# Row loads of two blocks, their normalization and one residual moved in a transformer block with routed experts

## The chip, the cores and the metric

The kernel runs on one core of a Trainium2 chip. The metric is the device time of one execution in microseconds (us). Three executions of the kernel before gave 1010.34, 1008.1 and 1010.42 us, median 1010.34. The profile comes from one further execution of 1009.59 us, whose span from the first to the last instruction is 1007.8 us.

Engines are named as the profile names them: PE (matrix multiplications and transposes), PEld (its weight loads), DVE, ACT and POOL (element-wise work), SP (which here only issues transfers). Each has a list of instructions of its own, in an order that the program fixes.

## The reference

The input x has 4 sequences of 1024 tokens with 256 features. All data are float32. What is computed, in short:

```python
z = layernorm(x)                      # the outer normalization
h = layer_norm(z)                     # ln1 of the attention
q, k, v = h @ wq, h @ wk, h @ wv      # 4 heads of 64
q = softmax(q * scale, axis=-1)       # over the features of a head
k = softmax(k * scale, axis=-2)       # over the 1024 tokens of a sequence
context = einsum('bhnd,bhne->bhde', k, v)
x1 = z + einsum('bhnd,bhde->bhne', q, context) @ wo + bo
x2 = x1 + gelu(layer_norm(x1) @ w_ff1 + b_ff1) @ w_ff2 + b_ff2
x3 = x + layernorm(x2 @ w_d + b_d)
# then: eight low-rank experts, two per token, on layernorm(x3);
out = x3 + layernorm(experts(rms_norm(layernorm(x3))))
```

The softmax of k runs over a whole sequence, so the context of a sequence needs all of its tokens.

## The kernel before, in words

**Tiling.** The 4096 tokens are cut into 8 blocks of 512 tokens; blocks 0 and 1 are the first sequence, 2 and 3 the second, and so on. A block is a tile of 128 partitions x 4 tokens x 256 features. Numbers at the end of a tile's name in this text are the block (z_2 is the tile z of block 2).

**Streams.** The program is written as Python generators, here called streams. `front(i)` takes the rows z_i of block i, normalizes them, transposes them (tiles pt_h, then hT), computes q and k (pq, pk), the exponentials, the transposes of q and k (pt_q, pkt) and the products of k with z (pz). At the second block of a sequence it makes the context and folds it into one matrix, mix (pzk, pctx, pmix). `middle(i)` loads the rows a second time (x_i, line 796), makes the normalized residual x1_i from them on ACT (line 806), multiplies q with mix (pa, line 821 adds it), and runs the feed-forward part (pf, py). `tail` makes the routing inputs. `prepare_q`, `prepare_attn`, `prepare_ff` and `prepare_ranks` prepare weights (for the second: pv, pw; for the third: pwt, pwdt, pbdt, pwdg, pwd, pbd, pbf, pc).

**What sets the order.** A planner in the program decides at build time which stream takes its next step. Each step adds to an estimated clock: `now()` for PE, `V`, `A`, `G` for DVE, ACT and POOL. A stream that yields a number waits until that estimated time; one that yields a function waits until the function is true. For data that come by transfer the planner holds estimates: the table `ARRIVE` for the first loads, and `now() + 2.5` for the later ones. What comes out is a fixed order of instructions on each engine. On the chip semaphores hold an instruction until its inputs are there, and everything behind it on that engine waits with it.

**Transfers.** SP issues the weights in this order: wff2 (line 201), wd, bd, wff1, w1 (1 MB each but wd and bd), eight pieces of b1 (line 185, 64 KB each), w3 (1 MB), eight pieces of b3, w2 (1 MB), eight pieces of b2; then the rows x_0 and x_1 of the residual (line 796, 512 KB each), and then, as buffers come free, z_2, x_2, x_3, z_3 and so on. The program gives the transfers of SP and ACT eight semaphores in turn, so a transfer is issued only when the one eight places before it has landed.

**Buffers.** Pool `zp` has two buffers for z, so z_2 is loaded (line 170) when z_0 is no longer needed, that is after pz_0; z_3 after pz_1. Pool `sp` has two buffers with the tag "row" that hold x_2 and x_3 in this phase. There are eight PSUM banks, handed out to the matrix products in turn by `psum`.

**Lines that matter below.** 351 to 369: normalization of z on DVE and ACT (POOL makes the reciprocal root, line 354). 611: copies to hT on ACT. 635: exponential of q. 657 and 658: maximum and copy of k. 672: exponential of k. 703 and 715: copies of the transposed q and k. 765: mix. 796, 806, 821: rows, normalized residual and sum in `middle`.

Of the kernel before, what the change touches and what calls it, by code (L numbers as in the profile page):

```python
# [15 lines left out]
P = 128  # L16
# [49 lines left out]
def sandwich_kernel(  # L66
# [98 lines left out]
        return ap[i * BLK : (i + 1) * BLK, :].rearrange("(p t) d -> p t d", t=TB)  # L165

    def load_z(i):
        zs[i] = zp.tile([P, TB, D], F32, tag="z", name=f"z_{i}")
        if i > 1:
            nc.sync.dma_start(out=zs[i], in_=tokens(x, i))  # L170
            return
        for t, eng in ((0, nc.sync), (HT, nc.scalar)):
            eng.dma_start(out=zs[i][:, t : t + HT, :], in_=tokens(x, i)[:, t : t + HT, :])
# [29 lines left out]
    nc.sync.dma_start(out=wd_s[:, :, 0:D], in_=wd.rearrange("(c p) f -> p c f", p=P))  # L203
    bd_s = wp.tile([P, DX], F32, tag="bd_s", name="bd_s")
    nc.sync.dma_start(out=bd_s[:, 0:D], in_=bd.partition_broadcast(P))
    wff1_s = load_w(nc.sync, wff1, [P, DC, FF], "wff1_s", "(c p) f -> p c f", p=P)
    w1_s = load_w(nc.sync, w1, [P, DC, FF], "w1_s", "(c p) f -> p c f", p=P)
    b1_s = load_ranks(b1, "b1_s")
    w3_s = load_w(nc.sync, w3, [P, DC, FF], "w3_s", "(c p) f -> p c f", p=P)
# [15 lines left out]
    def now():  # L225
        return pe[0] / 2400.0 + idle[0]
# [50 lines left out]
    def calm():  # L277

        return free["V"] - 0.5
# [130 lines left out]
        return read_out(e)  # L410


    ARRIVE = {"z0": 4.3, "z1": 9.1, "wqv": 8.6, "wff2": 14.6, "wff1": 18.0}

    def prepare_q():

# [55 lines left out]
    def prepare_ranks():  # L472
# [21 lines left out]
        for t, r_, n in ((a13_s.rearrange("p c (a k) -> p (c a) k", a=2),  # L494
# [6 lines left out]
                A(0.25 + n * STRIP / 1000.0)  # L501
            yield 0.0

    def prepare_ff():
        yield ARRIVE["wff2"]
        wff2T = mp1.tile([P, DC, FF], F32, tag="actB", name="wff2T")
        for c in range(DC):
            for h in range(2):
                pt = psum(f"pwt_{c}_{h}")
                for j in range(4):  # L510
                    flip(pt[:, j * P : (j + 1) * P], wff2_s[:, h * 4 + j, c * P : (c + 1) * P])
                nc.scalar.copy(wff2T[:, c, h * BLK : (h + 1) * BLK], pt)
                e = read_out(A(0.6, now() + 0.2))
                yield 0.0

        wdT = mp2.tile([P, DC, D], F32, tag="m1", name="wdT")
        bdT = mp2.tile([P, D], F32, tag="wt", name="bdT")
        pt = psum("pwdt")
        for e_ in range(DC):
            for c in range(DC):  # L520
                flip(pt[:, e_ * D + c * P : e_ * D + (c + 1) * P], wd_s[:, c, e_ * P : (e_ + 1) * P])
        nc.scalar.copy(wdT.rearrange("p e d -> p (e d)"), pt)
        read_out(A(0.6, now() + 0.2))
        pt = psum("pbdt")
        for c in range(DC):
            flip(pt[:, c * P : (c + 1) * P], bd_s[:, c * P : (c + 1) * P])
        nc.scalar.copy(bdT, pt[:, 0:D])
        e = read_out(A(0.45, now() + 0.2))
        yield e
        pw = psum("pwdg")  # L530
        for e_ in range(DC):
            g = wq_s[:, e_, D:DX]
            for c in range(DC):
                mm(pw[:, c * E : (c + 1) * E], wdT[:, e_, c * P : (c + 1) * P], g,
                   e_ == 0 and c == 0, False, skip_group_check=True)
            mm(pw[:, DC * E : (DC + 1) * E], bdT[:, e_ * P : (e_ + 1) * P], g, False, e_ == DC - 1,
               skip_group_check=True)
        nc.vector.tensor_copy(
            wd_s[:, :, D:DX], pw[:, 0 : DC * E].rearrange("p (c e) -> p c e", e=E)
        )  # L540
        nc.vector.tensor_copy(bd_s[:, D:DX], pw[:, DC * E : (DC + 1) * E])
        yield read_out(V(0.25, now() + 0.2))
        for f in range(FC):
            pw = psum(f"pwd_{f}")
            for c in range(DC):
                mm(pw[:, 0:DX], wff2T[:, c, f * P : (f + 1) * P], wd_s[:, c, :], c == 0, c == DC - 1)
            nc.vector.tensor_copy(wff2d_s[:, f, :], pw[:, 0:DX])
            read_out(V(0.4, now() + 0.2))
            yield 0.0

        pw = psum("pbd")
        for c in range(DC):
            mm(pw[:, 0:DX], vcol(V_BFF2, c).to_broadcast([P, P]), wd_s[:, c, :], c == 0, c == DC - 1)
        nc.vector.tensor_tensor(bd_s, bd_s, pw[:, 0:DX], ALU.add)
        read_out(V(0.4, now() + 0.2))
        yield 0.0
        yield ARRIVE["wff1"]

        pw = psum("pbf")
        for f in range(FC):  # L560
            for c in range(DC):
                mm(pw[:, f : f + 1], wff1_s[:, c, f * P : (f + 1) * P], vcol(V_LN2B, c),
                   c == 0, c == DC - 1)
        nc.vector.tensor_tensor(bff1_s, vec[:, V_BFF1 : V_BFF1 + FC], pw[:, 0:FC], ALU.add)
        read_out(V(0.15, now() + 0.2))
        for c in range(DC):
            nc.vector.tensor_scalar(
                wff1_s[:, c, :], wff1_s[:, c, :], vcol(V_LN2G, c), None, ALU.mult
            )
            yield V(1.2)  # L570
        for h in range(2):
            cols = slice(h * BLK, (h + 1) * BLK)
            centred([wff1_s[:, c, cols] for c in range(DC)], wff1_s, cols, f"pc1_{h}", 0.69)
            yield 0.0


    qTs, norms, mixes, kmaxes, ksums, kzs, xgs = {}, {}, {}, {}, {}, {}, {}
    summed, attended, stored = set(), set(), {}

    def front(i):  # L580
        b, h = divmod(i, BPB)

        def new(what, shape):


            pool, tag = {
                1: {"hT": (bp, "h2T"), "q": (mp1, "copy"), "k0": (gp, "g"), "k1": (gp, "g")},
                0: {},
            }.get(i if i < 2 else i % 2 * 3, {
                "hT": (mp2, "u0"), "q": (mp2, "tT"), "k0": (mp2, "act0"), "k1": (mp2, "act1"),  # L590
            }).get(what, (bp, what))
            return pool.tile(shape, F32, tag=tag, name=f"{what}_{i}")

        if i not in zs:
            load_z(i)
        z = zs[i]
        yield now() + 2.5 if i > 1 else ARRIVE[f"z{i}"]
        st, mv = tiles(f"in{i}")
        for js in ((0, 1), (2, 3)):
            stats(z, st, mv, js)  # L600
            yield calm()
        rr = small([P, TB], "rr", f"rr_x{i}", 3)
        yield rsqrt2(mv, 1e-5, 1e-5, rr, f"x{i}")
        norms[i] = mv
        yield lambda: i < 2 or i - 2 in summed
        lm, e = less_mean(mv, rr, f"z{i}")
        yield normalize(z, z, mv, rr, lm, e, "VAVA")
        hT = new("hT", [P, DC, BLK])

        def to_h(c, pt):  # L610
            nc.scalar.copy(hT[:, c, :], pt)

        yield from transposed(z, f"h{i}", to_h)
        yield lambda: zeroth.done

        q = new("q", [P, TB, DX])
# [20 lines left out]
            yield 0.0  # L637

        wide = small([P, TB], "wide", f"wide_{i}")
        nc.vector.reciprocal(wide, rr)  # L640
        yield lambda: i < 6 or 2 * i - 11 in turned
        xgs[i] = small([P, TB, E], "xg", f"xg_{i}", 6)
        nc.vector.tensor_tensor(
# [7 lines left out]
        for c in range(DC):  # L651
# [5 lines left out]
            nc.vector.tensor_reduce(kmax[:, c, h : h + 1], pk, AX.X, ALU.max)  # L657
            nc.scalar.copy(k, pk)
            read_out(max(V(0.7, now() + 0.2), A(0.6, now() + 0.2)))
            yield 0.0  # L660
        yield lambda: h == 0 or b in ksums

# [16 lines left out]
        else:  # L679
# [3 lines left out]
            nc.vector.tensor_tensor(less, kbias, kbias0, ALU.subtract)  # L683
            nc.scalar.activation(less, less, AF.Exp)
            e = A(0.2, V(0.15), "exp")
            nc.vector.tensor_tensor(ksum0, ksum0, less, ALU.mult)
            nc.vector.tensor_tensor(ksum, ksum, ksum0, ALU.add)
            nc.vector.reciprocal(ksum, ksum)
# [16 lines left out]
        for _ in transposed(q, f"q{i}", to_q):  # L705
            yield 0.0

        kt = new("q", [P, TB, D])
        for jj in range(0, TB, 2):
            pt = psum(f"pkt_{i}_{jj}")  # L710
# [5 lines left out]
            end = read_out(A(0.6, now() + 0.2))  # L716
            yield 0.0
        yield end
        yield lambda: h == 0 or i - 1 in summed
        pz = psum(f"pz_{i}")  # L720
        for c in range(DC):
            for n in range(TB):
# [70 lines left out]
    def middle(i):  # L793
# [1 line left out]
        xt = xts[i] = pool.tile([P, TB, RW], F32, tag=tag, name=f"x_{i}")  # L795
        nc.sync.dma_start(out=xt[:, :, 0:D], in_=tokens(x, i))
        yield now() + 2.5
        yield lambda: i // BPB in mixes and (i < 2 or i - 1 in flipped)
        qT, mix = qTs[i], mixes[i // BPB]
        _, r, e = rsqrt(norms[i], 1e-5, f"x{i}")  # L800
        pool, tag = (mp1, "actB") if i == 1 else (x1p, "x1")
        x1 = pool.tile([P, TB, D], F32, tag=tag, name=f"x1_{i}", bufs=1)
# [2 lines left out]
        for j in range(TB):  # L805
# [4 lines left out]
        nc.gpsimd.iota(xt[:, :, R_ID], pattern=[[1, TB]], base=i * BLK, channel_multiplier=TB,  # L810
                       allow_small_or_imprecise_dtypes=True)
        G(0.6)
        st, mv = tiles(f"x1_{i}")
        for jj in range(0, TB, 2):
            pa = psum(f"pa_{i}_{jj}")
# [11 lines left out]


        aside = {1: "u0", 3: "act", 5: "act"}.get(i)
        yield lambda: i < 2 or (i - 2 if i < 7 else i - 1) in fed  # L830
        yield lambda: aside != "act" or ranked.done

# [804 lines left out]

    EN = mybir.EngineType
    with tc.manual_schedule(engines={EN.PE, EN.DVE, EN.Activation, EN.Pool}):
        fronts = [  # L1640
            Stream(lambda i=i: i < 2 or i - 2 in summed,
                   lambda i=i: front(i))
            for i in range(NBLK)
        ]
        zeroth = Stream(always, prepare_q)
        first = Stream(always, prepare_attn)
        once = Stream(always, prepare_ff)
        ranked = Stream(always, prepare_ranks)
        blocks = [
            Stream(lambda i=i: i < 2 or (stored.get(AFTER[i]) == 2 if i in AFTER else i - 2 in attended),  # L1650
                   lambda i=i: middle(i))
            for i in range(NBLK)
        ]
# [13 lines left out]
        def sides():  # L1667

            yield from closing
            yield zeroth  # L1670
            yield from ready
            yield from tails
# [119 lines left out]
```

## Time and profile before

| what | value |
|---|---|
| profiled execution | 1009.59 us, span 1007.8 us |
| median of three executions | 1010.34 us |
| busy time of PE | 970.8 us (96%) |
| busy time of DVE, ACT, POOL | 452.2, 339.5, 416.6 us |
| PE busy in 0 to 36.49 us (up to the first pq of block 1) | 26.33 us |
| PE busy in 36.49 to 100 us | 57.76 of 63.51 us |
| PE busy in 100 to 330 us | 230.00 of 230.00 us |
| PE busy in 330 to 1007.8 us | 656.71 of 677.80 us |
| mean granted clock of PE | 0.991 |

How to read it: the row of a group gives the line of the kernel, the engine, the operation, the tile written and the tiles read, the count, the busy time and the idle time of the engine just before with what ended it. A row of the timeline begins with start and duration in us. "SPq" and "ACTq" are the transfer issues of those engines. PE's busy time counts also a matrix product that runs at half clock.

### The profile page before, as it was taken

The page shows a single profiled execution, that of the slowest core. Times are in us where ns is not written, and L with a number is a line of the kernel's source. Part 1 is how long each engine was busy: PE and PEld are TensorE (multiplying, and loading weights), DVE is VectorE, ACT ScalarE, POOL GpSimd, SP SyncE. Part 2 cuts the span into 40 slices and gives each one's busy share as a digit, 9 for nine tenths or more (in the row PEclk, how much of TensorE's full clock was granted, in tenths as well). Part 3 has the DMA queues.
Part 4 walks back from the last instruction along what each step waited for, and adds up shares of the span by engine and source line. Part 5 has one row for each costly group of instructions (what it writes and reads, how often), then busy time and mean ns, then how long its engine had stood idle before and what let it go on. Part 6 is the DMA issues. An engine that isn't in the chain of part 4 may idle for free. (4 is left out here: it accounts for less than half of the span.)

```text
span 1007.8 us, 12120 instructions
## 1 busy us (share of the span) xinstructions
PE 970.8 (96%) x4259; PEld 652.9 (65%) x4259; DVE 452.2 (45%) x1427; ACT 339.5 (34%) x702; POOL 416.6 (41%) x464
## 2 busy tenths in 40 slices
PE   6997999999999999998999999999999999999993
PEld 5776888888888888887764363543636446364453
DVE  5575575848574554745222324333233332332123
ACT  2424552353432222221213424345243442421110
POOL 2003001201212213232753847849387593866432
PEclk9999999999999999999999999999999999999997
DMA  8501800100202101121200110201111020100000
GB/s 286 180 22 31 189 26 22 59 27 1 86 3 83 44 19 47 65 70 31 68 10 0 43 44 26 64 6 49 37 43 43 0 65 1 43 32 21 1 0 23
DMA packets 30960, 48.01 MB, mean 48 GB/s; under 512 B 4176, under 2 KB 22704, under 8 KB 30896
## 3 DMA queue, kind: packets, MB, share of 16 engines
q1 hardware_dynamic: 20832, 32.15, 10.4%
q10 hardware_dynamic: 6992, 6.55, 2.7%
q0 software_dynamic: 3072, 8.51, 2.3%
q8 instruction: 35, 0.57, 0.2%
q14 instruction: 29, 0.24, 0.1%
HBM read 26.09 MB, written 17.17 MB: 43 GB/s over the span
## 5 line engine op out<-in xcount | busy, mean ns | idle before, releaser
L305 PE MATMUL ph<-tT,w_s 128*128 128x512 f32 (+1 forms) x576 | 235.6, 554 | 3.0 <-DVE act L1267 2.8
L305 PEld LDWEIGHTS ph<-tT,w_s 128*128 128x128 f32 x576 | 105.5, 190 | 124.8 <-issue 110.4
L305 PE MATMUL py<-wff2d,g 128*128 128x264 f32 x512 | 119.2, 386 | 0.0
L305 PEld LDWEIGHTS py<-wff2d,g 128*128 128x128 f32 x512 | 97.4, 190 | 16.5
L1267 DVE TENSOR_TENSOR act<-act,ph 128x512 f32<-128x512 f32 (+1 forms) x96 | 55.7, 595 | 104.2 <-PE ph L305 56.0
L1317 POOL TENSOR_TENSOR actA<-act,act 128x512 f32<-128x512 f32 x32 | 40.7, 1271 | 129.0 <-DVE act L1267 119.5
L1552 ACT COPY py<-ph 128x512 f32<-128x512 f32 x94 | 53.2, 571 | 120.5 <-PE ph L305 119.6
L305 PE MATMUL pf<-h2T,wff_s 128*128 128x256 f32 x384 | 87.1, 380 | 0.9 <-DVE h2T L854 0.9
L1259 ACT ACTIVATE act<-ph 128x512 f32<-128x512 f32 (+1 forms) x96 | 48.4, 521 | 115.1 <-PE ph L305 98.5
L305 PEld LDWEIGHTS pf<-h2T,wff_s 128*128 128x128 f32 x384 | 72.1, 190 | 12.4 <-issue 1.6
L1267 DVE TENSOR_TENSOR act<-act,py 128x512 f32<-128x512 f32 x48 | 32.9, 686 | 103.6 <-ACT act L1259 103.6
L879 ACT ACTIVATE g<-pf,bff 128x256 f32<-128x256 f32 x128 | 52.1, 475 | 72.8 <-PE pf L305 72.7
L305 PE MATMUL po<-w_s,actA 128*128 128x256 f32 x256 | 60.6, 384 | 0.6 <-ACT tT L1372 0.5
L904 DVE TENSOR_TENSOR y<-py,bd_s 128x264 f32<-128x264 f32 x32 | 13.8, 431 | 101.0 <-PE py L305 101.0
L305 PE MATMUL po<-w_s,actB 128*128 128x256 f32 x256 | 59.0, 379 | 0.0
L1078 POOL DMA_INDIRECT rows<-x,to x32 | 31.9, 998 | 63.9 <-DVE rsa_x L340 17.4
L305 PEld LDWEIGHTS po<-w_s,actA 128*128 128x128 f32 x256 | 46.9, 190 | 14.1 <-issue 7.2
L305 PEld LDWEIGHTS po<-w_s,actB 128*128 128x128 f32 x256 | 48.7, 190 | 11.2 <-issue 5.3
L305 PE MATMUL py<-u,bw 32*128 32x512 f32 x192 | 54.4, 640 | 0.0
L305 PE MATMUL ph<-u,bw 32*128 32x512 f32 x192 | 54.4, 640 | 0.0
L343 POOL TENSOR_TENSOR rs_y<-rsa_y,neghalf 128x2 f32<-128x2 f32 x16 | 11.4, 715 | 93.4 <-DVE rsa_y L340 86.2
L1317 POOL TENSOR_TENSOR actB<-act,act 128x512 f32<-128x512 f32 x31 | 39.6, 1278 | 21.9 <-DVE act L1267 21.9
(280 smaller groups left out, 1610.3 us busy)
## 6 DMA issues: line engine op xcount, KB each, us to landing
rows<-none ACTq DMA_DIRECT2D x4, 1052.0 KB, 13.9
kept<-x SPq DMA_DIRECT2D x8, 526.0 KB, 2.7
x<-in_x_dram SPq DMA_DIRECT2D x8, 512.0 KB, 3.8
row<-rows SPq DMA_DIRECT2D x7, 526.0 KB, 3.9
w_s<-in_w_dram SPq DMA_DIRECT2D x3, 1024.0 KB
z<-in_x_dram SPq DMA_DIRECT2D x6, 512.0 KB
bw<-b_s SPq DMA_DIRECT2D x24, 128.0 KB, 3.8
wff_s<-in_wff_dram SPq DMA_DIRECT2D x2, 1024.0 KB
```

Source lines behind the costliest of these rows:

```text
L305: nc.tensor.matmul(out_, lhsT=lhsT, rhs=rhs, start=start, stop=stop, **kw)
L343: nc.gpsimd.tensor_tensor(r, a, neghalf[:, 0:n], ALU.pow)
L879: nc.scalar.activation(g[:, k * W : (k + 1) * W], pf[:, k * W : (k + 1) * W], AF.Gelu_apprx_tanh, bias=bff1_s[:, f : f + 1],)
L904: nc.vector.tensor_tensor(y[:, j % HT, :], py[:, 0:DX], bd_s, ALU.add)
L1078: ins = nc.gpsimd.indirect_dma_start(out=dst[:, :], out_offset=bass.IndirectOffsetOnAxis(ap=at, axis=0), in_=src, in_offset=None, bounds_c ...
L1259: nc.scalar.activation(to, h, AF.Silu)
L1267: nc.vector.tensor_tensor(to, to, h3, ALU.mult)
L1317: lambda x0=x0, x1=x1, op=op: nc.gpsimd.tensor_tensor(ac, x0, x1, op))
L1552: nc.scalar.copy(py[a], ph[a])
```

## The change

1. `load_z(2)` and `load_z(3)` take the two "row" buffers of pool `sp` and are issued by SP in the prologue: z_2 ahead of wff1, z_3 ahead of w1. The planner's table gets the estimates 15.0 and 19.0 for them.
2. The normalization of z leaves `front` and becomes a stream of its own, `prelude(i)`. Blocks 1 to 3 are normalized by ACT alone ("AAAA"), with the product of mean and reciprocal root on POOL; blocks 0 and 4 to 7 stay with both engines ("VAVA").
3. `middle(i)` no longer waits for the context before it makes the normalized residual x1; it waits only for the statistics of the block (and an order among blocks), and asks for the context later, ahead of the products pa.
4. Some waits of the planner keep buffers safe in the new order (`keyed`, `folded`, `summed`).

```diff
     def load_z(i):
-        zs[i] = zp.tile([P, TB, D], F32, tag="z", name=f"z_{i}")
+        if i in (2, 3):
+            zs[i] = sp.tile([P, TB, RW], F32, tag="row", name=f"z_{i}")[:, :, 0:D]
+        else:
+            zs[i] = zp.tile([P, TB, D], F32, tag="z", name=f"z_{i}")
...
+    load_z(2)
     wff1_s = load_w(nc.sync, wff1, [P, DC, FF], "wff1_s", "(c p) f -> p c f", p=P)
+    load_z(3)
     w1_s = load_w(nc.sync, w1, [P, DC, FF], "w1_s", "(c p) f -> p c f", p=P)
...
-    ARRIVE = {"z0": 4.3, "z1": 9.1, "wqv": 8.6, "wff2": 14.6, "wff1": 18.0}
+    ARRIVE = {"z0": 4.3, "z1": 9.1, "wqv": 8.6, "wff2": 14.6, "z2": 15.0, "wff1": 18.0, "z3": 19.0}
...
+    def prelude(i):
+        if i not in zs:
+            load_z(i)
+        z = zs[i]
+        yield now() + 2.5 if i > 3 else ARRIVE[f"z{i}"]
+        st, mv = tiles(f"in{i}")
+        for js in ((0, 1), (2, 3)):
+            yield lambda: i < 2 or free["V"] < now() + 0.5
+            stats(z, st, mv, js)
+        rr = rrs[i] = small([P, TB], "rr", f"rr_x{i}", 3)
+        if 0 < i < 4:
+            lm = small([P, TB], "lm", f"lm_z{i}", 8)
+            nc.vector.tensor_scalar(lm, mv[:, :, 0], -1.0, None, ALU.mult)
+            V(0.15)
+            rsqrt2(mv, 1e-5, 1e-5, rr, f"x{i}")
+            nc.gpsimd.tensor_tensor(lm, lm, rr, ALU.mult)
+            e = G(0.5)
+            norms[i] = mv
+            yield lambda: 0 in heads if i == 1 else now() > e and free["A"] < now() + 1.5
+            zeds[i] = normalize(z, z, mv, rr, lm, e, "AAAA")
+        else:
+            yield rsqrt2(mv, 1e-5, 1e-5, rr, f"x{i}")
+            norms[i] = mv
+            yield lambda: i < 4 or i - 2 in summed
+            lm, e = less_mean(mv, rr, f"z{i}")
+            zeds[i] = normalize(z, z, mv, rr, lm, e, "VAVA")
...
     def middle(i):
...
         nc.sync.dma_start(out=xt[:, :, 0:D], in_=tokens(x, i))
         yield now() + 2.5
-        yield lambda: i // BPB in mixes and (i < 2 or i - 1 in flipped)
-        qT, mix = qTs[i], mixes[i // BPB]
+        yield lambda: i in norms and (i - 1 in flipped if i > 1 else i == 0 or folded)
         _, r, e = rsqrt(norms[i], 1e-5, f"x{i}")
...
         G(0.6)
+        yield lambda: i // BPB in mixes and i in qTs
+        qT, mix = qTs[i], mixes[i // BPB]
```

Lines of the changed kernel are later by 3 to 35: the residual's load is line 829, the residual line 838, the normalization line 380.

More of the change, by code (lines that the diff above doesn't have):

```diff
@@ L502, in prepare_ranks @@
             yield 0.0
+    folded = []
     def prepare_ff():
@@ L549, in prepare_ff @@
             yield 0.0
+        folded.append(True)
         pw = psum("pbd")
@@ L574, in prepare_ff @@
             yield 0.0
-    qTs, norms, mixes, kmaxes, ksums, kzs, xgs = {}, {}, {}, {}, {}, {}, {}
-    summed, attended, stored = set(), set(), {}
+    rrs, qTs, norms, mixes, kmaxes, ksums, kzs, xgs = {}, {}, {}, {}, {}, {}, {}, {}
+    keyed, summed, attended, stored = set(), set(), set(), {}
+    zeds, heads = {}, set()
+    def prelude(i):
[24 more added lines that the diff above has]
+            zeds[i] = normalize(z, z, mv, rr, lm, e, "VAVA")
     def front(i):
@@ L588, in new @@
                 0: {},
-            }.get(i if i < 2 else i % 2 * 3, {
+            }.get(i if i < 2 else 3 if i == 2 else i % 2 * 3, {
                 "hT": (mp2, "u0"), "q": (mp2, "tT"), "k0": (mp2, "act0"), "k1": (mp2, "act1"),
@@ L592, in new @@
             return pool.tile(shape, F32, tag=tag, name=f"{what}_{i}")
-        if i not in zs:
-            load_z(i)
+        yield lambda: i in zeds
         z = zs[i]
[L597 to L607, printed above, removed]
+        yield zeds[i]
         hT = new("hT", [P, DC, BLK])
@@ L611, in to_h @@
             nc.scalar.copy(hT[:, c, :], pt)
-        yield from transposed(z, f"h{i}", to_h)
+        for he in transposed(z, f"h{i}", to_h):
+            yield 0.0
+        heads.add(i)
+        yield he
         yield lambda: zeroth.done
@@ L639, in front @@
         wide = small([P, TB], "wide", f"wide_{i}")
-        nc.vector.reciprocal(wide, rr)
+        nc.vector.reciprocal(wide, rrs[i])
         yield lambda: i < 6 or 2 * i - 11 in turned
@@ L659, in front @@
             read_out(max(V(0.7, now() + 0.2), A(0.6, now() + 0.2)))
+            if c == DC - 1:
+                keyed.add(i)
             yield 0.0
@@ L685, in front @@
             e = A(0.2, V(0.15), "exp")
+            yield max(e, ke)
             nc.vector.tensor_tensor(ksum0, ksum0, less, ALU.mult)
@@ L706, in front @@
             yield 0.0
+        yield lambda: i != 3 or 2 in summed
         kt = new("q", [P, TB, D])
@@ L718, in front @@
         yield end
-        yield lambda: h == 0 or i - 1 in summed
+        yield lambda: i == 0 or i - 1 in summed
         pz = psum(f"pz_{i}")
@@ L829, in middle @@
         aside = {1: "u0", 3: "act", 5: "act"}.get(i)
+        yield lambda: aside != "u0" or 2 in keyed and 3 in summed
         yield lambda: i < 2 or (i - 2 if i < 7 else i - 1) in fed
@@ L1639, in sandwich_kernel @@
     with tc.manual_schedule(engines={EN.PE, EN.DVE, EN.Activation, EN.Pool}):
-        fronts = [
-            Stream(lambda i=i: i < 2 or i - 2 in summed,
-                   lambda i=i: front(i))
+        preludes = [
+            Stream(lambda i=i: i < 4 or i - 2 in summed, lambda i=i: prelude(i))
             for i in range(NBLK)
         ]
+        fronts = [Stream(always, lambda i=i: front(i)) for i in range(NBLK)]
         zeroth = Stream(always, prepare_q)
@@ L1649, in sandwich_kernel @@
         blocks = [
-            Stream(lambda i=i: i < 2 or (stored.get(AFTER[i]) == 2 if i in AFTER else i - 2 in attended),
+            Stream(lambda i=i: i < 2 or (stored.get(AFTER[i]) == 2 if i in AFTER else i - 2 in attended and i in summed),
                    lambda i=i: middle(i))
@@ L1669, in sides @@
             yield from closing
+            yield from preludes
             yield zeroth
```

## The prediction

> **What bounds the kernel now.** I read the share of busy time first, then PE's waits in the first 200 us, then busy time by stretch, then the timelines of SP and ACT. PE is busy 96% of the span.
>
> ```profile
> PE pcg L305 <- DVE gate_s L421: 8.7, 1, 8.7
> PE pt_h L318 <- DVE x L821: 4.1, 3, 1.4
> PE pt_q L318 <- DVE lm_x L360: 1.5, 1, 1.5
> PE pt_q L318 <- DVE lm_z L360: 1.4, 1, 1.4
> PE pmix L305 <- DVE cbd L757: 0.2, 1, 0.2
> ```
>
> These are PE's waits up to 200 us: in total, count, longest. The first is the start, which the change leaves alone. What it can win lies in the other four: 1.4 us at 26 us, and 4.1 + 1.5 + 0.2 = 5.8 us between 66 and 92 us. From 100 to 330 us PE has no idle time at all, and from the products pa of block 6 (329 us) PE's order is the same in both programs. The matrix instructions are the same in number and kind, and the array changes between whole, row and column use equally often. So the change is decided in the first stretch, and whatever PE loses there comes back nowhere: the end moves by the same amount.
>
> ```profile
> 11.02 10.28 SPq L185 DMA_DIRECT2D b_s<-in_b_dram  x8
> 21.34 0.42 SPq L177 DMA_DIRECT2D w_s<-in_w_dram  x1
> 21.81 6.55 SPq L185 DMA_DIRECT2D b_s<-in_b_dram  x8
> 28.48 1.44 SPq L177 DMA_DIRECT2D w_s<-in_w_dram  x1
> 29.96 5.80 SPq L185 DMA_DIRECT2D b_s<-in_b_dram  x8
> 35.81 1.35 SPq L796 DMA_DIRECT2D x<-in_x_dram  x2
> ```
>
> These are SP's issues. The residual's rows x_0 go out last, at 35.81 us, behind three weights of 1 MB and 24 small pieces. The trace's landing times for x are 3.8/5.5/7.3 us (least, median, most); x_0 is the first in an empty queue (1 to 5% DMA share at 35 to 37 us), so it lands at about 35.8 + 3.8 = 39.6.
>
> ```profile
> 20.23 0.63 ACT L635 ACTIVATE q<-q 128x512 f32<-128x512 f32 x1 [4.66 <-DVE q L631]
> ...
> 31.69 1.16 ACT L611 COPY hT<-pt_h 128x512 f32<-128x512 f32 x2
> ...
> 79.34 2.08 ACT L806 ACTIVATE x<-x,lm_x,rs_x 128x256 f32<-128x256 f32 x4 [2.21 <-DVE lm_x L360]
> ```
>
> ACT reads x_0 only at 79.34 us, 40 us after it landed, so that late load costs nothing before.
>
> **The moved residual.** In the changed program's order x1_0 (line 838) stands on ACT right behind the normalization of z_1, ahead of the exponentials of q_0, the copies and exponentials of k_0, the copies to hT_1, and all that follows. Its first instruction waits for the load of x_0, which SP still issues last. The planner counted 2.5 us for that load. ACT's order in the built program:
>
> ```
> 15 L380 Activation z_1_193<-z_1_193,lm_z1_317,rr_x1_316 128x256 x4
> 16 L838 Activation x1_0_286<-x_0_258,lm_x0_347,rs_x0_283 128x256 x4
> 17 L664 Activation q_0_354<-q_0_354 128x2x256 x2
> 18 L687 TensorCopy k0_0_387<-pk_0_0_388 128x512
> ```
>
> When does ACT get there? DVE ends the statistics of z_1 at 14.4; POOL's root takes 1.05 (line 354), its product perhaps 0.5 (an estimate between the iota's 0.14 and that root); four normalizations make 2.1, as the four of line 806 do: ACT is free at 18.4, with these steps' gaps of some 0.3.
>
> When does x_0 land? SP's small pieces each wait for an earlier transfer. The last of b1 goes out at 20.99, when w1 has landed; the last of b3 when w3 has (28.05); the last of b2 when w2 has (35.45); then x_0. The two new loads add 1.05 MB ahead of w1, while the queue moves 330 to 430 GB/s (8 to 18 us): 2.7 us. The chain behind keeps its lengths, so x_0 is issued at 38.5 and lands at 42.3. ACT stands from 18.4 to 42.3.
>
> What waits? After that ACT needs 2.1 for x1_0, 1.2 for two exponentials of q (0.63 each), 1.1 for two copies of k, 1.5 for its exponentials (24.74 to 26.26 before), 1.1 for the copies to hT_1: 7.0 us, and 0.2 to PE. The first pq of block 1 starts at 49.5. PE can do pq_0, pk_0, pt_h_1, pw and most of the weight transposes until 27.4 and then has nothing. DVE stands too, at the sums of q_0.
>
> How far behind is PE then? Before, pq of block 1 started at 36.5. But PE had by then also done pt_q_0 (0.90), pkt_0 (0.88), pwdg (1.25), two pwd (1.78) and pz_0 (3.46), by the differences of their starts: 8.3 us that the changed order has still ahead. So the lag is 49.5 - 36.5 + 8.3 = **21.3 us**, with the 1.4 us stall at 26 us contained in it.
>
> **What the rest wins and adds.** The other 5.8 us of stalls go: x1_0 is made long before its products, and z_2 and z_3 are at hand. New close pairs come: pmix_0 directly ahead of pa_0, where DVE's mix must come between (0.88 us, line 765, and the way there and back: 1.3); pkt_3 directly ahead of pz_3, with a copy between (0.8); pz_3 one product ahead of pzk_1, with DVE's sum between (0.4). Together +2.5. By bounds these may be 0, or as much as before (5.8).
>
> The clock: before, PE's granted clock is 0.50 for 3.4 us twice, at 53.8 (after pbf, 32 products with one column) and at 91.3 (after the stalls at 88 to 92); each costs 1.7. The second goes with its stalls, -1.7; pbf stays. After 22 us of idle PE starts cold. The row for that is the start of the profile: from 8.75 to 16.3 us pcg, pbq, pv, pt_h and pw take some 7.6 us, about twice what the same forms take later (eight pt_h 1.95 against 1.06, four products with 256 columns 1.75 against 1.03): a loss of up to 3.9. The two dips lost 1.7. I take 2.5, since some of the cold stretch falls on weight transposes still ahead of hT_1; bounds 0 and 3.9.
>
> The Trainium skill, "TensorE: Matmul & The Clock Gate", Part 1, gives one activity window of about 3.4 us at half clock after an idle one. By it the restart would cost 1.7 and the sum would be 0.8 lower.
>
> **Covered edits.** Six normalizations leave DVE (0.41 each, line 369) for ACT (0.5 to 0.6 each): after the stall ACT has 9.7 us of work (weight copies 3.0, q 1.2, qT and kt 2.2, k 1.2, z_2 2.1) beside 14.5 us of PE work up to pt_h_2 (pq 3.6, pt_q and pkt 1.8, pk 3.4, pz 3.5, pwdg 1.3, pwd 0.9); were it late, each copy would cost its 0.6. Three products on POOL come on (0.14 to 1.05 us each), where it idles 16.9 and 29.5 us between roots. The loads of x_2 and x_3 now wait for pz_2 and pz_3, which hold their buffers; z_4 and z_5 stand ahead of them on SP and wait for earlier ones, pz_0 and pz_1. x_2 would land some 4 us after pz_2; ACT wants it about 16 us later, so that is covered; if not, up to 7.3 us would show. wff1 comes some 1.5 us later and is used some 50 us after it lands.
>
> **Sum.** 21.3 - 5.8 + 2.5 - 1.7 + 2.5 = +18.8 us. Against the profiled execution of 1009.6 us (span 1007.8 and 1.8 around it) that is **1028.4 us**. The median shown is 0.7 above that execution, so a comparison might read 1029.
>
> **Rivals.**
> - *It works as meant, faster.* Its mechanism is an early x_0: ACT would pass x1_0 without standing and PE would keep its fill. The point: PE runs dry at 27.4 and needs 7 us of ACT ahead of that, so nothing is lost if x_0 lands by 20.5. Each us later costs one, and the gains (1.4 + 5.8 + 1.7 - 2.5 = 6.4) are used up at 27. If it landed by 20.5 the time would be 1009.6 - 6.4 = 1003. For it: only the statistics tie x1_0 down. Against it: the issue at 35.81 in the trace, and nothing in the diff moves it ahead. 4%.
> - *Smaller loss.* The two loads hide in SP's gaps and x_0 lands at 39.6 as before (-2.7), no new stall (-2.5), no cold start (-2.5): 1020.7. If pbf's dip goes too, 1019. For it: DMA is at 17 to 22% at 28 to 30 us. 23%.
> - *Larger loss.* Blocks 6 and 7 come later, and the feed-forward part has less beside it: stalls like those of before (+3.3), x_0 2 us later (a median landing of 5.5), the full cold start (+1.4), and a few waits of 1.3 us between 130 and 330 us (+4): 1039. 23%.
> - *Nothing visible.* ACT stands, but in time that the weights cost PE anyway: for that x_0 would have to land between 24 and 30 us. 2%.
>
> **Chances.** The forecast's own case (1023 to 1034) has 48%, the smaller and larger loss 23% each, faster 4%, no visible change 2%. The range takes in the bounds of the unknown terms, 1018 to 1039. Faster by over 0.3% 0.04, within 0.3% (about what a measurement of this kernel can tell from no change) 0.02, slower 0.94.
>
> **What would show it.** In the profile after: ACT idle for about 24 us ahead of line 838, ended by the transfer of x; that transfer issued by SP at about 38.5; PE empty from about 27 to 49; the first pq of block 1 at about 49.5; half clock after it; from then on about 2.5 us of stalls up to 130 us. It is wrong if x_0 lands early, if ACT's order has something ahead of line 838 that feeds PE, or if PE has idle time after 130 us that was not there.

## The result, and the profile after

The changed kernel takes 1023.16 us (median of 5 executions, 1022.23 to 1024.63), against 1010.37 us for the kernel before (5 executions, 1008.1 to 1011.65): a ratio of 1.013, 95% interval 1.0114 to 1.0147. The profiled execution took 1022.74 us, its span 1020.7 us, 12.9 us longer than before. The forecast was 1028.4 us: the direction and the place are right, the size is 5.2 us too large.

These are PE's waits up to 350 us in the kernel after: total, count, longest.

```profile
PE pwt L323 <- ACT k L687: 16.7, 1, 16.7
PE pcg L310 <- DVE gate_s L426: 8.7, 1, 8.7
PE pa L310 <- DVE mix L798: 0.6, 1, 0.6
PE pz L310 <- ACT q L748: 0.3, 1, 0.3
PE pwd L310 <- DVE wd_s L545: 0.3, 1, 0.3
```

The four stalls of before (1.5, 1.4, 4.1 and 0.2 us) are gone. One of 16.7 us has come: PE wants to transpose a weight and has no bank for it, because ACT has not yet copied k_0 out of its banks. The waits name the last link only; what held ACT up is seen in ACT's own timeline:

```profile
15.87 2.07 ACT L380 ACTIVATE z<-z,lm_z,rr_x 128x256 f32<-128x256 f32 x4 [0.34 <-POOL lm_z L605]
40.13 2.07 ACT L838 ACTIVATE x<-x,lm_x,rs_x 128x256 f32<-128x256 f32 x4 [22.19 <-DMA x<-in_x_dram]
...
45.52 1.05 ACT L637 COPY hT<-pt_h 128x512 f32<-128x512 f32 x2
```

ACT ends the normalization of z_1 at 17.94 us and stands for 22.2 us for the transfer of x_0. The copies of k and to hT_1, which feed PE, are queued behind. The transfer is late because of where it stands among SP's issues:

```profile
13.20 0.38 SPq L180 DMA_DIRECT2D w_s<-in_w_dram  x1
13.62 10.56 SPq L188 DMA_DIRECT2D b_s<-in_b_dram  x8
24.22 0.42 SPq L180 DMA_DIRECT2D w_s<-in_w_dram  x1
24.69 5.33 SPq L188 DMA_DIRECT2D b_s<-in_b_dram  x8
30.16 0.38 SPq L180 DMA_DIRECT2D w_s<-in_w_dram  x1
30.59 5.72 SPq L188 DMA_DIRECT2D b_s<-in_b_dram  x8
36.35 1.22 SPq L829 DMA_DIRECT2D x<-in_x_dram  x2
```

These are the issues of w1, b1, w3, b3, w2, b2 and of the rows x_0 and x_1. x_0 still goes out behind all weights, issued at 36.35 us (35.81 before), though w3 went out 2.9 us later than before (24.22 against 21.34). PE's timeline shows the gap and its end:

```profile
25.63 1.47 PE L323 MATMUL pwt<-ident,wff_s 128*128 128x128 f32 x12
43.77 1.11 PE L323 MATMUL pwt<-ident,wff_s 128*128 128x128 f32 x4 [16.67 <-ACT k L687]
44.68 1.06 PE L323 MATMUL pwdt<-ident,wd_s 128*128 128x128 f32 x4
...
46.14 4.21 PE L310 MATMUL pq<-wq_s,hT 128*128 128x264 f32 x10
```

PE is empty from 27.10 to 43.77. The trace's clock events put the granted clock to 0.50 at 29.18, in that gap, and back to 1.00 at 49.66: the first ten products pq take 4.21 us. From 130 to 330 us PE has no idle time, as before. So the whole difference lies before 130 us: PE is idle there for 26.5 us (15.9 before), +10.6, and is busy over the whole span for 973.2 us (970.8 before), +2.4, which is the same work at half clock. Together 13.0, against 12.9 in the span. Part of the 2.4 us lies at the start, which the prediction left out: full clock is first granted at 18.94 us (16.21 before), and pq of block 0 takes 5.89 us in place of 3.72. It should cost nothing by itself, as PE runs dry afterwards anyway.

### The profile page after: what moved, and what is told of

The parts are those of the page before. It is cut to its first block, busy times and chain, and to the rows that moved or that the text cites. A ratio compares the mean times of both kernels' runs of the same rounds, so it can differ in the third digit from the quotient of the medians.

```text
span 1020.7 us, 12127 instructions
## 1 busy us (share of the span) xinstructions
PE 973.2 (95%) x4259; PEld 653.7 (64%) x4259; DVE 449.9 (44%) x1421; ACT 339.6 (33%) x706; POOL 418.0 (41%) x467
## 5 line engine op out<-in xcount | busy, mean ns | idle before, releaser
L348 POOL TENSOR_TENSOR rs_x<-rsa_x,neghalf 128x4 f32<-128x4 f32 x16 | 16.8, 1053 | 114.2 <-DVE rsa_x L345 101.8
L1113 POOL DMA_INDIRECT rows<-x,to x32 | 32.2, 1005 | 71.1 <-DVE x L1078 24.4
```

Source lines behind the costliest of these rows:

```text
L348: nc.gpsimd.tensor_tensor(r, a, neghalf[:, 0:n], ALU.pow)
L1113: ins = nc.gpsimd.indirect_dma_start(out=dst[:, :], out_offset=bass.IndirectOffsetOnAxis(ap=at, axis=0), in_=src, in_offset=None, bounds_c ...
```

## Experiments

**The theory (A)**: the normalized residual stands on ACT ahead of what feeds PE and waits for x_0, which SP issues last; everything else in the change is a gain. **The rival (B)**: the wait for a bank is the cause by itself, or the two early loads delay what PE needs; then the loss stays when x_0 is early or the residual late.

### x_0 earlier: x0_early, x0_ahead_of_w3, x0_ahead_of_w2

All three are the changed kernel with one transfer moved on SP: x_0 right behind z_3 (ahead of w1), ahead of w3, or ahead of w2. The orders on PE, DVE, ACT and POOL are those of the changed kernel.

```diff
     load_z(3)
+    xts[0] = xp.tile([P, TB, RW], F32, tag="x", name="x_0")
+    nc.sync.dma_start(out=xts[0][:, :, 0:D], in_=tokens(x, 0))
     w1_s = load_w(nc.sync, w1, [P, DC, FF], "w1_s", "(c p) f -> p c f", p=P)
```

> The changed kernel with one transfer moved: the rows x_0 of the residual are issued by SP right behind z_3, ahead of w1, instead of behind all weights. The orders on PE, DVE and ACT are the changed kernel's. Theory A (ACT stands at the residual until x_0 has landed): x_0 lands at about 19 to 20 us, ACT has no wait over 3 us there, PE's 16.7 us wait at the weight transposes is gone, and with it the half clock after it (some 2 us): 1023.2 - 18.5 = about 1004.5 us, faster than before. Theory B (the eight PSUM banks, held by weight transposes that were moved ahead of pq of block 1, or the early loads of z_2 and z_3 themselves are what stops PE): the wait stays, and the time stays at 1018 to 1023 us.

> The changed kernel with x_0 issued behind the pieces of b1 and ahead of w3: issue at about 24.2 us, landing at 28 to 29 us, 11.5 us earlier than in the changed kernel. Theory A: time follows the landing one to one, so ACT's wait is about 10.5 us instead of 22.2, PE's wait about 5 us instead of 16.7, and the time about 1023.2 - 11.6 = 1011.6 us, near that of before. The forecast had the point where gain and loss are equal at a landing of 27 us. Theory B: no change, 1018 to 1023 us.

> The changed kernel with x_0 issued behind the pieces of b3 and ahead of w2: issue at about 30.2 us, landing at 34 to 34.5. Theory A (ACT stands until x_0 has landed, and time follows the landing one to one once PE is dry): the landing is 5.7 us earlier than in the changed kernel (40.1), so PE's wait is about 11 us and the time 1023.2 - 5.7 = 1017.5 us, on the line through the changed kernel and the run with x_0 ahead of w3.

| kernel | x_0 issued | ACT starts x1_0 | PE's wait there | median | ratio to before |
|---|---|---|---|---|---|
| x0_early | 12.95 | 22.29 | 1.0 | 1003.76 | 0.9941 [0.9929, 0.9953] |
| x0_ahead_of_w3 | 24.53 | 28.88 | 6.2 | 1012.76 | 1.0025 [1.0014, 1.0036] |
| x0_ahead_of_w2 | 31.04 | 35.56 | 12.7 | 1017.74 | 1.0079 [1.0064, 1.0094] |
| after | 36.35 | 40.13 | 16.7 | 1023.16 | 1.013 [1.0114, 1.0147] |

The times came near what was expected. One moved transfer of 512 KB turns a loss of 1.3% into a gain of 0.6%. In x0_early these are PE's longest waits up to 350 us, and ACT's row for the residual:

```profile
PE pcg L312 <- DVE gate_s L428: 8.9, 1, 8.9
PE pq L312 <- ACT hT L639: 1.0, 1, 1.0
```

```profile
22.29 2.08 ACT L842 ACTIVATE x<-x,lm_x,rs_x 128x256 f32<-128x256 f32 x4 [4.18 <-DVE xg L674]
```

The wait for a bank is gone, with the same banks and the same early loads: B falls.

One part of the expectation missed: x_0 was to land at 19 to 20 us with no wait over 3 us on ACT, and ACT stands for 4.18 us. The row names DVE's xg as what ended that wait, but the trace's landing events show the transfer: the last part of x_0 landed at 22.2 us, 9.3 us after its issue. (In x0_early_pbf_wide below the same row starts at 22.69, while xg is still running.) The queue moved 360 to 420 GB/s from 14 to 22 us; at the three later places the same 512 KB landed 3.8 to 4.5 us after their issue.

The table also gives the price of a late x_0. From x0_early to x0_ahead_of_w3 PE waits 5.2 us more, but the time grows by 9.0, and the span of the profiled executions by 9.4. The gap of 6.2 us also costs the clock: in x0_ahead_of_w3 it is 0.50 from 30.74 to 37.56 us (1.00 in x0_early), and PE is busy for 5.1 us of that, a loss of 2.5. The other 1.7 us are a stretch at half clock at 481 us, behind a wait of 2.8 us that x0_early has too, without such a stretch; they are no price of the late load (see the last section). From there on wait and time grow by 6.5 and 5.0, then by 4.0 and 5.4; the stretch at 481 us is absent from the last two.

### The planner told the truth: x0_estimate_true

The load stays last; the planner's estimate for it is 43 us, in place of 2.5 us after its issue.

```diff
-        yield now() + 2.5
+        yield now() + 2.5 if i else 43.0
```

> The changed kernel with one number changed: the planner's estimate for the landing of x_0 is 43 us instead of 2.5 us after the step. All transfers stay as they are; the planner then puts x1_0 on ACT behind the copy of mix_0 instead of behind the normalization of z_1. Theory A: the load is still late and costs nothing; ACT has no long wait, PE none after the start over 2 us: about 1004 us. Theory B (banks, or the early loads): PE still waits over 10 us at the weight transposes, 1018 to 1023 us.

Measured: 1012.62 us, ratio 1.0035 [1.0023, 1.0048]. Half of the expectation holds. The residual now stands on ACT at 76.14 us, nothing waits for x_0, and the wait of 16.7 us is gone, as A says. But the time missed: about 1004 was expected. PE's waits up to 350 us:

```profile
PE pcg L310 <- DVE gate_s L426: 8.7, 1, 8.7
PE pt_h L323 <- DVE x L855: 3.1, 2, 1.7
PE pz L310 <- ACT q L748: 2.7, 1, 2.7
```

By its own estimates the planner now makes x1_0 so late that DVE stands for it, and PE for DVE (3.1 us). In the other 2.7 us PE stands for ACT's copies of q, which are queued behind x1_1. Both are stalls of the old kind, 5.8 us together. The rest is clock. The busy time by stretches of 5 us (length, then PE, PEld, DVE, ACT and POOL with counts; the last columns are granted clock, DMA share and GB/s):

```profile
75.00:80.00 5.00, 1.94 (x16) 1.46 (x15) 2.62 (x7) 5.00 (x13) 0.00 (x0) 1.00 0.00 0
80.00:85.00 5.00, 5.00 (x25) 4.32 (x23) 2.40 (x11) 1.28 (x3) 1.26 (x2) 0.66 0.01 3
85.00:90.00 5.00, 5.00 (x29) 4.64 (x29) 0.83 (x2) 0.00 (x0) 0.86 (x2) 0.69 0.00 0
90.00:95.00 5.00, 5.00 (x19) 4.03 (x18) 0.46 (x1) 0.00 (x0) 0.00 (x0) 0.63 0.00 0
```

Behind the stalls PE is busy all the time and has on average a third of its clock less for 15 us: 5.1 us lost there ((0.34 + 0.31 + 0.37) x 5). The products pbf with one column stand in that stretch, from 83.96 to 87.95. Another 1.7 us go at 100 to 110 us (clock 0.90 and 0.76). Against x0_early, which has 2.2 us of such waits and one stretch that costs 1.7, that makes 3.6 us of waits and 5.1 us of clock more, 8.7 of the 8.9 us between the two kernels. So the true estimate takes the loss away that it was meant for, and the order that the planner then makes has losses of its own.

### The parts by themselves: context_first, residual_alone, residual_alone_x0_early

context_first is the changed kernel without part 3 (the residual waits for the context again); residual_alone is the kernel before with part 3 alone; residual_alone_x0_early adds the early x_0 to that.

```diff
-        yield lambda: i in norms and (i - 1 in flipped if i > 1 else i == 0 or folded)
+        yield lambda: i in norms and i // BPB in mixes and i in qTs and (i - 1 in flipped if i > 1 else i == 0 or folded)
```

> The changed kernel without its third part: the normalized residual again waits for the context in the planner; early loads and separate normalization streams stay. Theory A: the whole loss belongs to the third part, so this gives the gain of the first two alone, about 1003 to 1005 us, and ACT has no long wait. If the third part has a gain of its own beside its harm, this is slower by 1 to 2 us than the run with the true estimate. Theory B: 1018 to 1023 us.

> The kernel before with the third part alone: the normalized residual no longer waits for the context; no early loads of z_2 and z_3, no separate normalization. Theory A: x_0 is issued at 35.8 and lands at 39.6 as before; x1_0 stands on ACT ahead of the exponentials of q_0, so ACT stands from about 16 to 39.6 and PE is dry from about 26 to 45. PE's lag is some 18 us, some of the 5.8 us of stalls behind 66 us go and the restart costs about 2 us: 1022 to 1028 us. If the loss needed the early loads of z_2 and z_3 as well, this would stay within 1008 to 1012.

> The kernel before with the third part alone and x_0 issued ahead of w1. Theory A: no wait on ACT for x_0. The stalls that the trace of before had ahead of the transposes of x1_0 and x1_1 (4.1 + 1.5 us) go, and with them the second stretch at half clock (1.7): 1010 - 5 to 7 = 1003 to 1005 us. If it is the early rows z_2 and z_3 that fill PE, this gains less than 3 us.

- context_first: 1004.9 us, ratio 0.995 [0.9938, 0.9963], as expected. The early rows and the separate normalization are worth about 5 us by themselves; of the stalls 1.4 us (pt_q, for DVE's q) and 0.3 us remain. The expectation also asked whether part 3 has a gain of its own. Against x0_early, which has part 3 with little of its harm, the difference is 1.1 us and the intervals overlap, so no gain of part 3 is shown. (x0_estimate_true, named there for the comparison, is 7.7 us slower than context_first, for the losses of its own order.)
- residual_alone: 1032.69 us, ratio 1.0237 [1.022, 1.0254], above the expected 1022 to 1028. ACT stands 23.6 us for x_0, PE 18.7 us. The loss is larger than the whole change's because that wait is longer (16.7 in the changed kernel), because a stall of 3.4 us ahead of pt_h of x1 stays, and because half clock on a busy PE costs 8.3 us, against 4.7 in the changed kernel, by the clock events of the two traces (from the first event on).
- residual_alone_x0_early: 1009.8 us, ratio 1.0008 [0.9999, 1.0017]; 1003 to 1005 was expected, a miss; what came is the other case named there, that without the early rows z_2 and z_3 it gains less than 3 us. The long wait is gone, so the cause stands; but an early residual alone gains nothing. PE's waits up to 350 us are 1.9 us less than before, and half clock on a busy PE costs 1.6 us more. Rows of residual_alone (PE's longest wait and ACT's residual), then of residual_alone_x0_early (DVE around PE's remaining stall of 3.4 us, up to 81.24):

```profile
PE pt_q L318 <- DVE lm_z L360: 18.7, 1, 18.7
39.39 2.07 ACT L808 ACTIVATE x<-x,lm_x,rs_x 128x256 f32<-128x256 f32 x4 [23.64 <-DMA x<-in_x_dram]
```

```profile
76.08 0.65 DVE L829 TENSOR_TENSOR x<-x,pa 128x512 f32<-128x512 f32 x1
...
77.85 1.19 DVE L697 TENSOR_REDUCE qsum<-q 128x16 f32<-128x1024 f32 x1
79.07 0.25 DVE L698 RECIPROCAL qsum<-qsum 128x16 f32<-128x16 f32 x1
79.36 1.23 DVE L699 TENSOR_TENSOR q<-q,qsum 128x1024 f32<-128x1024 f32 x1
80.50 0.68 DVE L829 TENSOR_TENSOR x<-x,pa 128x512 f32<-128x512 f32 x1
```

Between the two halves of the sum x1 + pa (line 829) DVE does the softmax of q_2, 2.7 us, and PE waits for the second half. By this trace the stall comes from DVE's order and not from a late residual; no run changed that order alone. In the whole change DVE has six normalizations less, and the blocks lie otherwise.

### Half clock behind pbf: x0_early_pbf_wide, before_pbf_wide

In the kernels before, after and x0_early the granted clock falls to 0.50 right behind the 32 products pbf, though PE is busy there without a gap. The edit lets each of them stream 64 equal columns, of which one is used; once on top of x0_early, once on the kernel before.

```diff
-                mm(pw[:, f : f + 1], wff1_s[:, c, f * P : (f + 1) * P], vcol(V_LN2B, c),
-                   c == 0, c == DC - 1)
+                mm(pw[:, f * 64 : (f + 1) * 64], wff1_s[:, c, f * P : (f + 1) * P],
+                   vcol(V_LN2B, c).to_broadcast([P, 64]), c == 0, c == DC - 1)
```

> The run with x_0 ahead of w1, and in it the 32 products pbf stream 64 equal columns each instead of one, of which one is used. It tests whether it is the small activity of products with one column that halves the clock behind pbf. If so, no half clock behind pbf and pz_2 takes 3.6 instead of 5.4 us, 1.7 us gained if the wider products cost nothing (at 64 columns they should stay near the 0.11 us that one takes): about 1002 us. If the clock falls for another reason, as long as before or up to 2 us longer: 1004 to 1006.

> The kernel before with one edit: the 32 products pbf stream 64 equal columns, of which one is used, in place of one column. If the half-clock stretch behind pbf (3.4 us at clock 0.50, from 53.8 us) costs PE its 1.7 us to the end, the median falls by 1.7 us, to a ratio of about 0.9983, the stretch at 53.8 is gone and the products behind pbf start at the same time while the rest is earlier. Rival: the waits of PE for DVE at 66 to 92 us (5.8 us in the kernel before) end when DVE is done, and DVE does not depend on PE's clock in that stretch; then the 1.7 us are only a longer wait, the ratio is 1.000 and the waits sum to about 7.5 us. A third possibility: the stretch only moves to the next place where PE waits, with the same ratio of 1.000 but unchanged waits.

PE's timeline, x0_early first, then x0_early_pbf_wide:

```profile
80.47 3.63 PE L312 MATMUL pbf<-vec,wff_s 128*128 128x1 f32 x32
83.97 5.39 PE L312 MATMUL pz<-z,q 128*128 128x256 f32 x16
...
472.04 3.72 PE L312 MATMUL ph<-tT,w_s 128*128 128x256 f32 x16 [2.78 <-DVE act L1306]
```

```profile
80.87 3.68 PE L312 MATMUL pbf<-vec,wff_s 128*128 128x64 f32 x32
84.39 3.67 PE L312 MATMUL pz<-z,q 128*128 128x256 f32 x16
...
470.73 5.41 PE L312 MATMUL ph<-tT,w_s 128*128 128x256 f32 x16 [2.77 <-DVE act L1307]
```

64 columns cost the same as one (3.68 against 3.63), and the products behind them run at full clock. But no gain is shown at the end. x0_early_pbf_wide took 1001.93 us, ratio 0.9929 [0.9915, 0.9944], which overlaps x0_early's 0.9941 [0.9929, 0.9953]; before_pbf_wide took 1010.46 us, ratio 0.9998 [0.9989, 1.0008]. In the profiled execution of x0_early_pbf_wide PE is 1.3 us ahead at 88 us, still so at 326 us, and loses it at 470: the products ph behind a wait of 2.77 us run at half clock (5.41, the last line of the second view). The same wait, 2.78 us, was there in x0_early, and the products behind it ran at full clock (3.72, the last line of the first view).

That is one execution. Three of the six of x0_early_pbf_wide (1001.14 to 1001.29 us) are faster than any of the six of x0_early (from 1002.04), so a gain of a us or so is not excluded there.

In before_pbf_wide the stretch behind pbf is gone. At the products pa of block 6 PE is 0.5 us ahead (328.94 against 329.44): pbf itself started 0.4 us later than in the trace of before, pz_1 now waits 0.3 us for ACT, and the stretch at 91 us hits 0.5 us harder. The waits between 66 and 92 us are as before, so the rival that they would grow by 1.7 us falls. A new stretch stands at 477.89 to 481.30 us, behind a wait of 2.8 us that the kernel before has too. Of the three outcomes named beforehand this is nearest to the third, and the edit is worth nothing there that can be measured. The stretch did not come up at the next wait, though, but more than 380 us later; the last section shows on what that hangs.

## Why the prediction was right, and where its sizes were off

**The mechanism.** Each step that was named is in the trace: x_0 issued behind all weights, ACT standing ahead of line 838 for its transfer, PE filling up to 27.10 (27.4 forecast) and then empty, half clock after the gap, no new idle time from 130 to 330 us. The experiments show it as the cause: x_0 early takes the loss away, and part 3 alone brings it. The size was less well met: 1023.16 us is at the lower edge of the forecast's own case (1023 to 1034) and nearer to the smaller loss (1020.7) than to 1028.4.

**The lag: 21.3 forecast, 17.9 measured** (46.14 - 36.49 + 8.3). This is the term that was mis-sized, in two places.
- *Landing at 42.3; it was 40.1.* The step "The chain behind keeps its lengths, so x_0 is issued at 38.5" did not hold in the profiled execution. The shift of 2.7 us did reach w3 (2.9 measured), but from w3 to w2 it took 5.94 us (7.14 before) and from w2 to x_0 6.19 (7.33 before): 2.3 us were given back, and x_0 went out 0.5 us later than before. The other runs show that half of this is spread between executions. Three kernels have the changed kernel's order on SP up to x_0 (after, x0_estimate_true, context_first): x_0 went out at 36.35, 37.24 and 38.51 us. Three have that of before (before, before_pbf_wide, residual_alone): 35.81, 34.96 and 35.09. On average that is 2.1 us later, against 2.7 forecast. Only the link from w3 to w2 is shorter in each of the first three (5.8 to 6.3 us against 7.1 to 7.9); from w2 to x_0 both groups lie between 6.2 and 7.3. Why the one link is shorter is open. A chain of transfers whose issues wait for landings isn't a fixed delay line.
- *7.2 us from the landing to pq; it was 6.0.* The step "7.0 us, and 0.2 to PE" added the durations of the rows. But they overlap: x1_0 lasts 2.07 and the next row starts 1.98 after it, and so on. And pq needs the first copy to hT_1 only. Differences of starts are the thing to add: 45.52 - 40.13 = 5.4, and 0.6 for that copy.

**The old stalls, -5.8: right.** All of them are gone (the 1.4 us at 26 us are in the lag).

**The new stalls, +2.5: 1.2 measured.** pmix to pa 0.6 (1.3 forecast), 0.3 at the copy of pkt (0.8), and 0.3 at pwd, which was not named; the 0.4 at pzk did not come.

**The dips, -1.7: right.** One stretch is gone, the one behind pbf stays: pz_2 takes 5.39 us (3.62 at full clock) behind it, at 103.49.

**The cold restart, +2.5: 1.9 measured.** The first 12 products pq take 4.66 us, against 2.79 at full clock (three quarters of 3.72). The transposes from 43.77 to 46.14 ran at half clock too, but beside ACT's copies. The Trainium skill, "TensorE: Matmul & The Clock Gate", Part 1, counts one window of about 3.4 us at half clock after an idle one, hence its 1.7; here the clock stayed at 0.50 for 5.9 us after PE began again (43.77 to 49.66): 2.5 us to the next border of the 3.41 us windows of the last section, and one more window. Of the 2.9 us lost in that time only what lay on the path cost.

The measured terms give 17.9 - 5.8 + 1.2 - 1.7 + 1.9 = +13.5, against 12.9 in the span. Of the 5.3 us that the forecast was above this, 3.4 are the lag, 1.3 the new stalls and 0.6 the restart.

**The rivals.** "Smaller loss" (1020.7) was right that x_0 lands about as before, 40.1 against its 39.6, but not in its reason: the two loads did not hide in SP's gaps, they put w3 off by 2.9 us, and the chain behind made 2.3 of it good in this execution. "It works as meant" was right about its condition: it put the turning point at a landing of 27, and between the rows of x0_early and x0_ahead_of_w3 (ACT's start at 22.29 and 28.88) a straight line reaches x0_early's own comparison time of 1009.85 us at 26.7. The line is steeper than the one to one that was counted (9.0 us of time for 6.6), for the clock and the stretch at 481 us, so the match is in part luck. Its time, 1003, is that of x0_early within a us.

## What to carry to other kernels

When a step is moved ahead on an in-order engine, ask of each of its inputs when it really lands, transfers first: a load that was harmless at the end of the queue becomes the bound once its reader stands ahead of the work that feeds the busiest engine. Here the loss went both when the landing was made early and when the step was undone. The two cures are not told apart here (1003.76 us for the moved issue, 1004.9 for the undone step, overlapping intervals), and the step by itself won nothing that was shown. A place early in the queue isn't an early landing either: x_0 took 9.3 us in the full queue. A planner's flat estimate for a load (2.5 us here, against a landing that was 22 us later than its reader) should be replaced by the place in the queue, yet a true estimate does not by itself give a good order (1012.62 against 1003.76 us). Add starts, not durations, when a chain is priced, and count a long gap on PE as the gap and some us of clock on top (1.5 to 2.9 us of busy time lost behind the gaps of 6.2 to 18.7 us here, 1.9 of 2.9 on the path in the changed kernel).

## What the runs showed of the hardware beyond that

- **A busy PE can lose its clock.** Behind 32 products with one column (3.5 to 3.6 us without a gap) the clock is 0.50 for about 3.4 us; with 64 columns, at the same duration, it stays at 1.00. In the nine traces with one column 2.45 to 3.24 us of these products fell into one window (see the next point), and half clock followed in all; in before_pbf_wide 2.61 us of the wide ones fell into one window, and it did not. The Trainium skill, "TensorE: Matmul & The Clock Gate", Part 1, speaks of how busy PE has been; by these runs what streams through the array counts, not whether an instruction is running.
- **The same gap may or may not cost the clock, and the traces show on what it hangs.** From the first to the last clock event of each of the eleven traces, the events lie whole multiples of 3.41 us apart (stretches at half clock of 3.41, 6.83, 13.65, 17.07 and 20.48 us). So each execution can be cut into windows of 3.41 us that end at its clock events. A wait of 2.77 or 2.78 us, ph for DVE, stands between 467 and 499 us in all eleven. In five of them a border of the windows falls inside it so that no window holds more than 1.75 us of it: full clock behind. In the other six one window holds 2.01 us or more: half clock in the window behind it. Over all windows at full clock between 20 and 970 us, the 21 with 1.0 to 1.75 us of idle time were followed by full clock and the 16 with 1.83 us or more by half. The Trainium skill, in the same section, says that the window runs freely. These traces fit that: their first clock event lies anywhere from 15.76 to 18.94 us, so a stretch at such a wait can come and go without any change to the order of instructions there. No run moved the windows on purpose.
- **The spread between executions has steps of this size.** The 15 executions of the kernel before that ran beside before_pbf_wide fall into two groups: 1008.38 to 1008.95 us at a mean granted clock of 0.994, and 1009.53 to 1010.95 at 0.991. The medians of the groups lie 1.4 us apart, near the 1.7 us that one stretch of 3.4 us at half clock costs. That it is one stretch more is an inference, since there is no trace of each.
